# Loading six chunk numbers early and moving two small writes to ScalarE's queue at a loop's entry

## The chip, the cores and the metric

The kernel runs on one core of a Trainium2 chip. The metric is the device time of one execution in microseconds. Before the change three runs took 746.41, 743.29 and 744.07 us, median 744.07.

The core's engines each run their own list of instructions: TensorE (PE in the profile, with PEld for its weight loads), VectorE (DVE), ScalarE (ACT), GpSimd (POOL) and SyncE (SP). [...] An engine that issues a DMA spends about 0.3 us on it in its own list, and the list behind it waits as long. An engine meets another's results through semaphores, and so does the completion of a DMA reach the engines.

## The reference

Four graph layers work on one graph of N = 2708 nodes with 128 features each. Each layer normalises the rows (`h = max(layernorm(x), 0)`) and adds the layer's result to x. The adjacency matrix `adj` holds zeros and ones.

- Layer 0 is an attention layer with weights `adj.T * exp(max(0.2 C, C))`, divided by their sum in each row.
- Layer 1 is a graph convolution with symmetric degree scaling.
- Layer 2 is a mean over neighbours with a second linear map and a batch norm.
- Layer 3 decides here. With `XW = h @ W` and scores `s_col`, `s_row` of its rows:

```
den = exp(leaky_relu(s_row[:, None] + s_col[None, :], 0.01))
num = adj @ den
att = where(num != 0, den / num, 0)
out = x + adj @ (att @ XW)
```

`adj @ den` is a product of two matrices of 2708 x 2708. Since `den` depends on a sum of two scores through a function of two slopes, sorting the nodes by score turns most of each row of `num` into two prefix sums.

## The kernel before

The kernel first reads the adjacency matrix and its transpose as float32, packs them to 8 bits (`adj8_d`, `adjt8_d` in DRAM) and computes layers 0 to 2 with TensorE. Columns are worked on in six blocks of 512 (`E0`, the last has 148).

**Ranking and the sums' stage.** For layer 3 the nodes are ranked by score and split into NC = 22 chunks of CH = 124. The stage around lines 1246 to 1630 sums the adjacency rows of each chunk with weights (`sums`, `last_sums`), turns these sums into prefix sums over the chunks (`prefixes`, `flatten`) and stores them in two parts (`pre_hi`, `pre_lo`). The columns are done in three pairs of blocks, (0, 3), (1, 4) and (2, 5). `store_pre(i)` handles pair i: four writes into the small tensor `early_d[i]` (line 1524), four into the full tensor `pre_d` (line 1530), and then four reads from `early_d[i]` (line 1535) that put the prefix rows straight into the first two row tiles of the loop. Of the four early writes, h = 0 go to SP's queue and h = 1 to ScalarE's.

**Row tiles.** A row tile `r` of the loop (44 in all, number q) has 128 partitions. 124 hold adjacency rows, fetched by an indirect DMA on POOL's queue (`fetch_into`, line 1445) as 8 bits and widened by VectorE (`widen`, line 1479). The last four hold prefix rows from the chunk before it. Which chunk that is is known only on the device: `chunk_of(q)` (line 1459) loads the number from the tile `pre_i` into a register of SP, computes with it and asserts its bounds, and the DMA that follows takes its address from the register. For q = 0 and 1 this is done in the sums' stage (`first_chunks`). For q from 2 on `fetch_pre(q)` (line 1682) does it, each time right ahead of the read of `pre_d`.

**The loop.** Its 22 steps s use row tiles 2s and 2s + 1. In each, TensorE multiplies densities (`d_hi`, `d_lo`) by the two row tiles, one block of columns after the other (line 1737), ScalarE takes the logarithm (`ln`, line 1738) and inverts it (line 1705), VectorE forms `e` (line 1711), and two steps later TensorE multiplies `e` by the fetched `xw` (line 1693). Step 0 takes its blocks in the order 0, 3, 1, 4, 2, 5, as the pairs come. At the end of step s the row tiles 2s + 6 and 2s + 7 are fetched. Row tiles 2 to 5 have their prefix rows fetched ahead of the loop. Their gathers differ: 2 and 3 are fetched in the sums' stage, 4 and 5 inside step 0 after its third block, since VectorE first copies their indices (line 1748).

**The proof tiles.** The kernel also verifies that the adjacency matrix holds only zeros and ones. For that it reads it tile by tile into `chk` (line 699) and compares on VectorE (line 695). In the loop one such tile is read in each odd step, by ScalarE's queue after the third block, and compared in the next even step, ahead of later work of VectorE.

**Order.** The instructions of the sums' stage run on each engine in the order written (`in_order`), and in the loop the marked ones (`pin`) do. The order between the engines' DMAs, and which of a small set of completion semaphores each one gets, is fixed when the program is built.

Of the kernel before, what the change touches and what calls it, by code (L numbers as in the profile page):

```python
# [20 lines left out]
def binary(  # L21
# [21 lines left out]
    nc = tc.nc  # L43
# [1412 lines left out]
    def chunk_of(q):  # L1456
        traced = nc.cur_bb.bb.instructions
        n = len(traced)
        chunk_before = nc.sync.value_load(pre_i[0:1, q : q + 1], min_val=0, max_val=NC - 1)
        load = traced[n]  # L1460
        issued = next(i for i in reversed(traced[:n]) if i.engine == load.engine and "DMA" in type(i).__name__)
        tc.add_manual_dep(
            load,
            issued.name,
            mybir.DependencyInfo(mybir.DependencyClass.NoSync, mybir.DependencyReason.DATA),
            reason="chunk_of",
        )
        return chunk_before
# [3 lines left out]
    def fetch_into(q, pool):  # L1472
        g = pool.tile([P, N], U8, tag="g8", name="g8", bufs=4 if pool is rows8_pool else 2)
        pin(gather(g[:CH], adjt8_d[:, :], row_i2[:CH, q - 4 : q - 3] if q in (4, 5) else row_i[:CH, q : q + 1]))
        rows8[q] = g
# [4 lines left out]

    for q in range(4):
        fetch_into(q, rows8_pool)
    first_chunks = [chunk_of(q) for q in range(2)]
    for q in range(2):
        rows_r[q] = plan.tile([P, N], F32R, tag="wide3", name="r", bufs=3)

# [28 lines left out]
    def store_pre(i):  # L1515
        pair = (i, i + 3)
        pre_hi = merge.tile([P, 512], F32, tag="pre_hi", name="pre_hi", bufs=2)
        pre_lo = merge.tile([P, 512], F32, tag="pre_lo", name="pre_lo", bufs=2)
        ts_(pre_hi[:W108].bitcast(I32), flat[:W108].bitcast(I32), -4096, None, ALU.bitwise_and)
        nc.vector.tensor_sub(pre_lo[:W108], flat[:W108], pre_hi[:W108])  # L1520
        parts = [(o, h, part_sb) for o, part_sb in ((0, pre_hi), (2 * NC, pre_lo)) for h in range(2)]
        wide = [E0[b][1] - E0[b][0] for b in pair]
        for o, h, part_sb in parts:
            (nc.scalar if h else nc.sync).dma_start(
                early_d[i][o : o + 2 * NC, h * 512 : h * 512 + wide[h]].bitcast(F32),
                part_sb[64 * h : 64 * h + 2 * NC, : wide[h]],
            )
        for o, h, part_sb in parts:
            lo, hi = E0[pair[h]]
            nc.sync.dma_start(pre_d[o : o + 2 * NC, lo:hi].bitcast(F32), part_sb[64 * h : 64 * h + 2 * NC, : wide[h]])  # L1530
        early_rows = early_d[i].rearrange("(f c) n -> f (c n)", c=NC).bitcast(F32)
        for q in range(2):
            for h, b in enumerate(pair):
                lo, hi = E0[b]
                nc.sync.dma_start(
                    rows_r[q][CH:, lo:hi].bitcast(F32),
                    early_rows[:, bass.ds(first_chunks[q] * 1024 + h * 512, hi - lo)],
                )
# [40 lines left out]
    with in_order():  # L1579
# [20 lines left out]
        diagonal(0)  # L1600
        flatten(0, p0)
        store_pre(0)
        last_sums(1)
        p = bank()
# [14 lines left out]
        flatten(1, p1)  # L1619
        last_sums(2)  # L1620
        store_pre(1)
        evacuate(2)
        cp4 = spread_c(4)
# [4 lines left out]
        nc.scalar.activation(sig, c_tab, AF.Exp, scale=0.99)  # L1628
        flatten(2, p2)
        store_pre(2)  # L1630

    prep.close()
# [42 lines left out]
    def fetch_pre(q):  # L1675
        if q % 6 < 2:
            r = plan.tile([P, N], F32R, tag="wide3", name="r", bufs=3)
        else:
            r = steps.tile([P, N], F32R, tag="r", name="r", bufs=4)
        rows_r[q] = r  # L1680
        chunk_before = chunk_of(q)
        pin(nc.sync.dma_start(r[CH:, :].bitcast(F32), pre_rows[:, bass.ds(chunk_before * N, N)]))

    def fetch_xw(s):
# [13 lines left out]
    for q in range(2, 6):  # L1698
        fetch_pre(q)
# [16 lines left out]
    for s in range(NE):  # L1716
# [45 lines left out]
        for q in (2 * s + 6, 2 * s + 7):  # L1762
            if q < NS:
                fetch_pre(q)
# [460 lines left out]
def kernel(tc, *args):  # L2225
    nc = tc.nc
    with tc.tile_pool(name="verdict", bufs=1) as verdict:
        flag = verdict.tile([1, 1], I32, name="flag")
        binary(tc, flag, *args)
        other = nc.values_load(flag[0:1, 0:1], min_val=0, max_val=1, skip_runtime_bounds_check_because="0 or 1")  # L2230
        with tc.If(other > 0, preferred_fallthrough_block=False):
            general(tc, *args)
# [32 lines left out]
```

## Time and profile before

| What | Value |
|---|---|
| Median of three runs | 744.07 us |
| Profiled execution, its own time | 746.78 us |
| Profiled execution, span of its instructions | 744.9 us |
| TensorE busy | 654.9 us (88%) |
| VectorE busy | 584.5 us (78%) |
| ScalarE busy | 467.6 us (63%) |
| Mean granted TensorE clock | 0.962 |
| DMA traffic | 146.99 MB, 197 GB/s in the mean |

The page divides the span into 40 slices. The loop's entry lies in slices 23 to 26 (from about 428 us). The chain of waits goes back from the last instruction to what released it, at each step. A line of a timeline gives the start, the duration, the engine with a q where its queue only issues, the line of the kernel, the operation, what it writes and reads, and how many were merged. A waits line gives who waited for what: microseconds in total, how many times, and the longest. A windows line gives a stretch, its length, each engine's busy time, the granted clock, the share of the 16 DMA engines in use and the rate.

### The profile page before, as it was taken

The page shows a single profiled execution, that of the slowest core. Times are in us where ns is not written, and L with a number is a line of the kernel's source. Part 1 is how long each engine was busy: PE and PEld are TensorE (multiplying, and loading weights), DVE is VectorE, ACT ScalarE, POOL GpSimd, SP SyncE. Part 2 cuts the span into 40 slices and gives each one's busy share as a digit, 9 for nine tenths or more (in the row PEclk, how much of TensorE's full clock was granted, in tenths as well). Part 3 has the DMA queues.
Part 4 walks back from the last instruction along what each step waited for, and adds up shares of the span by engine and source line. Part 5 has one row for each costly group of instructions (what it writes and reads, how often), then busy time and mean ns, then how long its engine had stood idle before and what let it go on. Part 6 is the DMA issues. An engine that isn't in the chain of part 4 may idle for free.

```text
span 744.9 us, 8701 instructions
## 1 busy us (share of the span) xinstructions
PE 654.9 (88%) x2777; PEld 418.3 (56%) x2777; DVE 584.5 (78%) x1021; ACT 467.6 (63%) x694; POOL 218.0 (29%) x198
## 2 busy tenths in 40 slices
PE   6889888868899988866898976899999999999994
PEld 4433333415678766644455634556666666657784
DVE  5999968967876896654799974499789989858972
ACT  5765667648775653426575455668888888765442
POOL 3320000131110210004570427156666766000000
PEclk9999998999999999997999997989999999999998
DMA  9699999766731699600100248857887777568702
GB/s 336 253 384 416 424 428 399 265 242 220 292 119 71 204 305 349 208 0 14 44 22 2 65 128 134 174 153 153 180 176 170 174 173 169 151 220 330 260 30 57
DMA packets 49131, 146.99 MB, mean 197 GB/s; under 512 B 12686, under 2 KB 26930, under 8 KB 40658
## 3 DMA queue, kind: packets, MB, share of 16 engines
q1 hardware_dynamic: 29740, 87.76, 34.5%
q10 hardware_dynamic: 4714, 34.68, 14.0%
q0 software_dynamic: 14624, 23.92, 13.1%
q8 instruction: 24, 0.39, 0.2%
q14 instruction: 29, 0.24, 0.1%
HBM read 126.55 MB, written 19.73 MB: 196 GB/s over the span
## 4 chain that ended last, share of the span: by engine, by line
PE 48%; issue 15%; DVE 13%; DMA 9%; ACT 6%; POOL 2%; SPq 0%; ACTq 0%; POOLq 0%; DVEq 0%
PE bank L1737 13%; PE acc L1693 12%; PE acc L614 7%; PE acc L1860 5%; DMA chk<-in_adj_t_dram 4%; PE acc L1252 3%; DVE chk L695 2%; DMA adj_d<-a 2%; DVE m L483 2%; ACT adjt L216 2%; PE acc L1117 1%; ACT y L474 1%; POOL adj_d L372 1%; DVE r L1479 1%; POOL rstd L157 1%
## 5 line engine op out<-in xcount | busy, mean ns | idle before, releaser
L1737 PE MATMUL bank<-r,d_hi 128*128 128x512 f32 (+1 forms) x264 | 143.1, 546 | 14.7 <-DMA r<-pre_d 6.5
L1693 PE MATMUL acc<-e,xw 128*128 128x512 f32 (+1 forms) x264 | 121.8, 549 | 0.0
L1738 ACT ACTIVATE ln<-bank,tiny 128x512 f32<-128x512 f32 x132 | 83.9, 636 | 57.6 <-PE bank L1737 47.1
L340 PE MATMUL acc<-tau,hw 128*128 128x512 f32 (+1 forms) x240 | 99.7, 562 | 13.2 <-DVE tau L348 13.2
L1445 POOL DMA_INDIRECT g<-adjt_d,row_i x44 | 93.2, 2117 | 30.9 <-DVE r_hi L1439 10.7
L1737 PE MATMUL bank<-r,d_lo 128*128 128x512 f32 (+1 forms) x264 | 100.3, 385 | 0.0
L481 ACT CAST m<-a 128x660 fp32r<-128x660 fp8e4 (+1 forms) x45 | 55.2, 1234 | 51.7 <-PE acc L1860 30.7
L340 PEld LDWEIGHTS acc<-tau,hw 128*128 128x128 f32 x240 | 43.5, 193 | 71.2 <-issue 43.9
L695 DVE SCALAR_TENSOR_TENSOR chk<-chk 128x2708 f32<-128x2708 f32 (+1 forms) x22 | 65.5, 2978 | 21.4 <-DMA chk<-in_adj_t_dram 21.4
L348 DVE SCALAR_TENSOR_TENSOR tau<-row_b,sg,a 128x1536 f32<-128x1536 f32 (+1 forms) x44 | 70.8, 1623 | 13.3 <-DMA a<-in_adj_dram 13.2
L1711 DVE SCALAR_TENSOR_TENSOR e<-row_b,sig,ln 128x1536 f32<-128x1536 f32 (+3 forms) x46 | 71.4, 1558 | 11.2 <-PE bank L1737 8.3
L1737 PEld LDWEIGHTS bank<-r,d_hi 128*128 128x128 f32 x264 | 51.5, 195 | 51.1 <-issue 27.0
L1479 DVE CAST r<-g 124x2708 fp32r<-124x2708 fp8e4 x44 | 70.9, 1651 | 7.5 <-DMA r<-pre_d 7.5
L371 ACT ACTIVATE a<-a 128x2708 fp8e4<-128x2708 f32 x22 | 54.1, 2458 | 25.5 <-issue 13.3
L1737 PEld LDWEIGHTS bank<-r,d_lo 128*128 128x128 f32 x264 | 51.6, 196 | 29.2 <-issue 24.0
L1705 ACT ACTIVATE ln<-ln 128x512 f32<-128x512 f32 (+2 forms) x68 | 62.9, 927 | 0.7 <-ACT ln L1738 0.7
L157 POOL TENSOR_TENSOR rstd<-isq,neg_half 128x4 f32<-128x4 f32 (+1 forms) x24 | 28.8, 1200 | 117.4 <-DVE isq L156 73.3
L1445 POOL DMA_INDIRECT xw<-xw_d,xw_i x22 | 35.9, 1631 | 70.4 <-PE acc L1693 57.4
L483 DVE CAST m<-a 128x2048 fp32r<-128x2048 fp8e4 (+1 forms) x43 | 39.5, 920 | 21.3 <-PE acc L614 11.7
L1693 PEld LDWEIGHTS acc<-e,xw 128*128 128x128 f32 x264 | 48.4, 191 | 12.8 <-issue 3.8
L614 PE MATMUL acc<-m,y_hi 128*128 128x512 f32 (+1 forms) x132 | 50.8, 391 | 4.8 <-ACT m L481 1.9
L614 PE MATMUL acc<-m,h_hi 128*128 128x512 f32 (+1 forms) x132 | 53.8, 415 | 0.1
(449 smaller groups left out, 1237.0 us busy)
## 6 DMA issues: line engine op xcount, KB each, us to landing
a<-in_adj_dram SPq DMA_DIRECT2D x21, 1354.0 KB
adjt<-in_adj_t_dram ACTq DMA_DIRECT2D x12, 1354.0 KB
chk<-in_adj_t_dram ACTq DMA_DIRECT2D x11, 1354.0 KB
chk<-in_adj_t_dram SPq DMA_DIRECT2D x10, 1354.0 KB
a<-in_adj_t_dram SPq DMA_DIRECT2D x9, 1354.0 KB
adj_d<-a POOLq DMA_DIRECT2D x22, 338.5 KB, 8.3
adjt_d<-adjt SPq DMA_DIRECT2D x5, 1354.0 KB
a<-adj_d SPq DMA_DIRECT2D x5, 1024.0 KB
```

Source lines behind the costliest of these rows:

```text
L340: nc.tensor.matmul(accs[b][:, : hi - lo], stationary, tau[b // 3][:, o : o + hi - lo], start=first, stop=last)
L348: nc.vector.scalar_tensor_tensor(tau, row_b[:, h0:h1], sg[:, t : t + 1], tiles_a[t][:, h0:h1], ALU.max, ALU.mult)
L481: nc.scalar.copy(m[:, : hi - lo], src[:, lo:hi])
L614: nc.tensor.matmul(sums_of[phase, b][:, : hi - lo], part[:, t, :], tiles_m[k][:, lo - base : hi - base], start=t == 0 and i == 0, stop=t = ...
L695: lambda: nc.vector.scalar_tensor_tensor(a[:r], a[:r], 1.0, a[:r], ALU.is_equal, ALU.not_equal, accum_out=odd[:r, t : t + 1])
L1445: return nc.gpsimd.indirect_dma_start(out=out, out_offset=None, in_=src, in_offset=bass.IndirectOffsetOnAxis(ap=idx, axis=0),)
L1479: pin(nc.vector.tensor_copy(rows_r[q][:CH], g[:CH]))
L1693: m = nc.tensor.matmul(ys_acc[b][:, : hi - lo], xws[s], waiting[s][:, lo:hi], start=(s == 0), stop=(s == NE - 1))
L1705: pin(nc.scalar.activation(lns[s][:, lo:hi], lns[s][:, lo:hi], AF.Exp, scale=-1.0))
L1711: nc.vector.scalar_tensor_tensor(waiting[s][:, lo:hi], row_b[:, lo:hi], sig[:, s : s + 1], lns[s][:, lo:hi], ALU.max, ALU.mult)
L1737: pin(nc.tensor.matmul(num[:, : hi - lo], d, a[:, lo:hi], start=(j == 0), stop=(j == 3)))
L1738: pin(nc.scalar.activation(lns[s][:, lo:hi], num[:, : hi - lo], AF.Ln, bias=tiny))
```

## The change

Six chunk numbers, not two, are loaded into SP's registers in the sums' stage, behind the last DMA that SP issued before and after `pre_i` is ready. `fetch_pre` for row tiles 2 to 5 uses these registers and loads nothing. All four early writes of the third column pair are issued by ScalarE; those of the first two pairs stay as they were.

```
@@ -1480,7 +1480,7 @@
     for q in range(4):
         fetch_into(q, rows8_pool)
-    first_chunks = [chunk_of(q) for q in range(2)]
+    first_chunks = [chunk_of(q) for q in range(6)]
     for q in range(2):
         rows_r[q] = plan.tile([P, N], F32R, tag="wide3", name="r", bufs=3)
@@ -1521,7 +1521,7 @@
         for o, h, part_sb in parts:
-            (nc.scalar if h else nc.sync).dma_start(
+            (nc.scalar if h or i == 2 else nc.sync).dma_start(
                 early_d[i][o : o + 2 * NC, h * 512 : h * 512 + wide[h]].bitcast(F32),
                 part_sb[64 * h : 64 * h + 2 * NC, : wide[h]],
             )
@@ -1678,7 +1678,7 @@
         rows_r[q] = r
-        chunk_before = chunk_of(q)
+        chunk_before = first_chunks[q] if q < 6 else chunk_of(q)
         pin(nc.sync.dma_start(r[CH:, :].bitcast(F32), pre_rows[:, bass.ds(chunk_before * N, N)]))
```

More of the change, by code (lines that the diff above doesn't have):

```diff
@@ L1482, in binary @@
         fetch_into(q, rows8_pool)
-    first_chunks = [chunk_of(q) for q in range(2)]
+    first_chunks = [chunk_of(q) for q in range(6)]
     for q in range(2):
@@ L1523, in store_pre @@
         for o, h, part_sb in parts:
-            (nc.scalar if h else nc.sync).dma_start(
+            (nc.scalar if h or i == 2 else nc.sync).dma_start(
                 early_d[i][o : o + 2 * NC, h * 512 : h * 512 + wide[h]].bitcast(F32),
@@ L1680, in fetch_pre @@
         rows_r[q] = r
-        chunk_before = chunk_of(q)
+        chunk_before = first_chunks[q] if q < 6 else chunk_of(q)
         pin(nc.sync.dma_start(r[CH:, :].bitcast(F32), pre_rows[:, bass.ds(chunk_before * N, N)]))
```

## The prediction

> **What bounds the kernel now.** I read the page's slices first, then the chain of waits where the loop starts, the windows of the loop's steps, and the waits of SP's queue.
>
> From 500 us on, the loop of 22 steps is TensorE's own: a step takes 9.64 us without idle time. The change touches nothing there, so what counts is when step 5 starts (499.63). The chain of waits just before (start, length, what):
>
> ```profile
> 445.00 1.59 DMA r<-early_d
> ...
> 446.64 0.76 PE bank L1737 x2
> ...
> 447.55 0.49 SPq L1459
> ...
> 448.52 6.82 DMA r<-pre_d
> 455.48 1.21 PE bank L1737 x2
> ...
> 459.77 20.54 DMA chk<-in_adj_t_dram
> ...
> 485.05 2.97 DVE r L1479 x2
> 488.06 1.22 PE bank L1737 x2
> ```
>
> The reader is to see three links. A chunk load (L1459) stands ahead of row tile 3's read of `pre_d`; that read, issued at 448.52, takes 6.8 us, and step 1 waits for it until 455.48. ScalarE issues the transfer of the proof tile `chk` in the middle of step 1, at 459.77. It lands at 480.3, and VectorE then needs 7.7 us (L695, `e`, two widenings) until step 4 runs in full at 488.06.
>
> The windows of steps 1 to 5, matmuls of L1737 alone:
>
> ```profile
> core 0: us, PE busy (x) PEld busy (x), PEclk, DMA share, GB/s
> ...
> 450.30:462.40 12.10, 8.02 (x24) 5.44 (x24) 0.64 0.90 152
> 463.20:472.85 9.65, 8.12 (x24) 4.29 (x25) 1.00 1.07 192
> 472.85:485.20 12.35, 7.82 (x24) 4.22 (x24) 1.00 0.80 157
> 486.60:499.63 13.03, 10.55 (x24) 5.21 (x25) 0.75 0.60 172
> 499.63:509.27 9.64, 8.13 (x24) 4.32 (x25) 1.00 0.49 123
> ```
>
> Step 2 is a clean 9.65; steps 3 and 4 lose 7.5 us together, against 2 x 9.63 from 472.85 to a possible 492.1. Step 4 also runs at clock 0.75. The DMA engines are full meanwhile (0.90, 1.07).
>
> SP's queue, around the change (start, length, what):
>
> ```profile
> 438.08 3.33 SPq L1535 DMA_DIRECT2D r<-early_d  x4
> 441.51 0.31 SPq L1524 DMA_DIRECT2D early_d<-pre_hi  x1
> 441.91 0.31 SPq L1524 DMA_DIRECT2D early_d<-pre_lo  x1
> 442.27 0.73 SPq L1530 DMA_DIRECT2D pre_d<-pre_hi  x2
> 443.05 0.75 SPq L1530 DMA_DIRECT2D pre_d<-pre_lo  x2
> 444.06 1.99 SPq L1535 DMA_DIRECT2D r<-early_d  x4
> 447.22 4.23 SPq L1682 DMA_DIRECT2D r<-pre_d  x4
> ```
>
> The four last reads take 4.23 us because each has a chunk load in front of it. What SP waits for, in total, how often, the longest:
>
> ```profile
> SPq L1682 <- DMA chk<-in_adj_t_dram: 15.2, 1, 15.2
> ...
> SPq L1535 <- DMA early_d<-pre_hi: 1.7, 1, 1.7
> ```
>
> Neither reader needs that data: the trace shows SP's and ScalarE's DMAs taking turns on eight completion semaphores, and a DMA that gets one in use waits. Moving two writes to ScalarE can therefore move a wait on SP.
>
> **The change, part by part.**
>
> *Four chunk loads earlier.* The loads for q = 0 and 1 stand at 415.37 and 416.18 and are over at 416.78: 0.81 and 0.60 us each, made of the load itself (0.28 to 0.46), its address (0.15) and an assertion (0.02). Four more take 2.4 to 3.2 us, to 420 at the latest. SP's next work is at 429.03, after a wait of 12.2 us for `pre_hi`: cover enough, cost nothing. If that cover were gone they would cost these 3.2 us. The change issues no more DMAs in all.
>
> *The same four loads gone from the entry.* The spacing of the four reads is 1.30 us (448.52 to 449.81); without load, address and assertion (0.81 us) it is 0.47. So row tile 2 is read 0.9 us sooner and row tile 3 1.7 us sooner, apart from the next edit.
>
> *Two early writes of the third pair off SP.* They took 441.51 to 442.27, so what follows moves 0.76 us forward. They go out on ScalarE at 438.70 and 439.4 rather than 441.5 and 441.9, so their data is there before SP reads it. ScalarE pays two issues of 0.30 us: the first in the stretch where it waits for `pre_lo` (438.70 to 439.06), the second ahead of step 0's first logarithm, 439.43 to 439.77. Behind that stands TensorE's third block, 440.17 to 440.5, which stops until 442.25 anyway for a read of the second pair. Cost nothing; without that stop, 0.34 us. VectorE has no new wait; POOL's queue is passed by nothing.
>
> *The semaphore turns.* One of the second pair's reads waits 1.7 us, to 440.7, for a third-pair write on ScalarE. With four such writes the first read may wait too. Bounds: no wait at all (1.7 us gained) and all four reads behind 440.7 (438.08 becomes 440.7, and the last ends 0.9 us later). I take 0.5 us of loss, nearer the second, since the one wait that shows is of that sort. So the gathers of row tiles 4 and 5, released by step 0's third block at 446.5, go at 447.0. They have slack: both are widened by 461.2, and step 2 started at 463.24.
>
> *Step 1.* Row tile 3's read goes at 448.52 - 1.7 - 0.76 + 0.5 = 446.6. It needs the writes of `pre_d`, whose last is issued at 443.2 and takes the 2.3 us that an early write takes in the chain (435.55 to 437.88): 445.5, no stop. How long does it take? Row tile 2's read took 3.1 us (447.22 to TensorE's 450.32), before gather packets filled the engines; row tile 3's took 6.8, among them. Ends: 449.7 and 453.4. At 446.6 it is ahead of the gathers, so I take 449.7 to 450. Step 1 is then 5.5 us sooner (2.1 at the other end).
>
> *The transfer of `chk`.* Its issue follows step 1: 459.77 - 5.5 = 454.3. The landing moves by 0 to 5.5 us: nothing if the engines, at a share of 0.85 or more from 452 us on, have no room; 5.5 if it lands as long after its issue. I take 3.5, since the packets of its queue took 65% of the engines between 464 and 472 us and the gathers' 29%: where it competes, it wins. It lands at 476.8. [...]
>
> *Step 4.* VectorE's 7.7 us after the landing gives 484.5 in place of 488.06: 3.5 us. Without a late transfer, step 4 can start when step 3 ends, at 482.5: 5.5 us.
>
> *The clock.* From 488.06 to 499.63 step 4 needed 11.57 us, 1.9 more than a warm step: half clock after TensorE's idling between 482 and 488. With some 2 us idle instead of 5 I take 1.4 of it back (ends 0 and 1.9). [...] The window after 452 us, at 0.50, agrees that idling costs clock.
>
> **Sum.** 0 (early loads) + 0 (ScalarE) + 3.5 + 1.4 = 4.9 us, all of it at step 5's start; from there the loop and the last product run as before. The profiled execution took 746.78 us by its own time (span 744.9 and 1.9 around it), 2.7 above the median of the three runs, 744.07. So 741.9 for that execution, and 744.07 - 4.9 = 739.2 as the forecast. About 0.5% (3.7 us) is what a measurement tells from no change.
>
> **Rivals.**
>
> *The gain stays in the entry.* Step 1 starts early, but `chk` lands 0 to 2 us sooner, because the DMA engines are full from 452 to 480 us. For it: shares 0.85 to 1.15 in those windows. [...] Also here: row tile 3's read is slow wherever it goes (6.8 us), which moves step 1 by 2.1 only. Time 744.07 - 0 to 2.5, say 742.5.
>
> *Slower: the early `chk` starves the gathers of row tiles 4 and 5.* They land 11.1 to 11.5 us after issue now; the slowest of the eight, issued among the transfer's packets, needed 23.8. Today the transfer's packets come after 462 us, when these two have landed (458.0 and 459.3). From 456 us they would run into them. With 23.8 us, tile 5 lands at 471.5 or later, is widened by 474.6, and step 2 starts 11.4 us late. Step 5 then starts at 474.6 + 3 x 9.64 = 503.5, 3.9 later than now: 748.0. It decides from 469 us on for tile 5's landing; sooner than that the step-4 stall that goes pays for it. Against it: they are nearly done by 457.
>
> *The change does not do what it says.* The waits list also holds one of TensorE (0.2 us) for row tile 2's read at 447.4; were it real, that read stays at 447.2 and tile 3's comes at 447.7. It would still be 0.8 us sooner, 743 or a little less.
>
> **How the numbers follow.** Forecast (3.7 us or more gained): 0.55, own range 735.5 to 740.3, the low end being 5.5 + 1.9 and another 1.2 from steps 2 and 3 moving forward. Gain stays in the entry: 0.22; the change does not do what it says: 0.05. Slower by starved gathers: 0.18. These give the chances of faster, same (0.22 + 0.05) and slower. The range, 735.5 to 746.0, leaves out some 0.05 below and about 0.13 of the slow case above.
>
> **What would show it.** Right: the four reads of L1682 within 2 us from about 446; step 1's full start near 450; the `chk` issue near 454; step 3 without a stop, step 4 at clock 0.9 or more, step 5's start near 494.7. Wrong: `chk` landing at 479 or later; a long stop at step 2 behind widening (starved gathers); SP stopped before the second pair's reads beyond 441.5.

## The result and the profile after

The changed kernel takes 755.76 us (median of four runs, 750.76 to 758.33) where the kernel before takes 744.21 in the same comparison: a ratio of 1.0128, 95% interval 1.0087 to 1.017. It is slower by about 1.3%; the forecast was 739.2 and its range ended at 746.0. A ratio leaves out executions that took over 1.5% more than the fastest of the same kernel; this concerns kernel 11 below alone, where it leaves out three of ten.

The profiled execution took 753.69 us by its own time (span 751.8), 6.9 more than the one before. The loop begins 1.8 us earlier in this trace, and the loop's entry loses 8.5 us: counted from the first matmul of L1737, step 5 starts at 71.8 us in place of 63.3, and from there to the end it is 245.4 us in one trace and 245.3 in the other. Below, "at t = ..." means microseconds after that first matmul (434.52 in this trace, 436.33 before).

The windows of step 0 to step 5, matmuls of L1737 alone, in the changed kernel (columns as before):

```profile
core 0: us, PE busy (x) PEld busy (x), PEclk, DMA share, GB/s
434.52:448.83 14.31, 8.73 (x24) 5.63 (x25) 0.76 0.35 98
448.83:457.29 8.46, 7.53 (x24) 5.21 (x24) 0.80 0.89 130
457.29:466.37 9.08, 0.00 (x0) 0.03 (x1) 0.68 1.04 217
466.37:487.11 20.74, 10.88 (x24) 5.34 (x25) 0.65 0.47 83
487.11:496.73 9.62, 8.12 (x24) 4.31 (x25) 1.00 0.50 115
496.73:506.36 9.63, 8.13 (x24) 4.31 (x25) 1.00 0.90 171
```

Step 1 is what the change promised: 8.46 us instead of 12.10. Steps 3 and 4 are clean at 9.62 and 9.63, without the stop that the proof tile caused before. Everything is lost between them: 9.08 us in which TensorE multiplies nothing, and a step 2 of 20.74 us. Step 2 pays for the stop twice: between 461 and 481 us the granted clock is 0.50.

What step 2 waits for stands in the chain of waits of the changed kernel:

```profile
446.08 1.30 POOL g L1445
...
447.69 25.68 DMA g<-adjt_d,row_i
473.44 1.58 DVE r L1479
475.06 1.22 PE bank L1737 x2
```

It is the gather of row tile 5, which takes 25.7 us after its issue. In the kernel before, the gathers of row tiles 4 and 5 stand so among the DMA issues (the last number is the microseconds from issue to landing):

```profile
g<-adjt_d,row_i POOLq DMA_INDIRECT x1, 11.5
```

```profile
g<-adjt_d,row_i POOLq DMA_INDIRECT x1, 11.1
```

VectorE's widenings in the changed kernel show that row tile 4 is late too (in brackets the idle time ahead of each, and what ended it):

```profile
464.70 1.57 DVE L1479 CAST r<-g 124x2708 fp32r<-124x2708 fp8e4 x1 [14.64 <-DMA g<-adjt_d,row_i]
473.44 1.57 DVE L1479 CAST r<-g 124x2708 fp32r<-124x2708 fp8e4 x1 [7.17 <-DMA g<-adjt_d,row_i]
```

Row tile 4 was issued at 446.08 and landed at 464.6, which is 18.5 us against 11.5 before. These are two delays, the second landing 8.7 us behind the first, and the experiments are about what makes each. SP's queue and POOL's around them in the changed kernel, then POOL's in the kernel before:

```profile
439.30 1.62 SPq L1535 DMA_DIRECT2D r<-early_d  x4
441.02 0.70 SPq L1530 DMA_DIRECT2D pre_d<-pre_hi  x2
441.85 0.69 SPq L1530 DMA_DIRECT2D pre_d<-pre_lo  x2
443.06 1.65 SPq L1535 DMA_DIRECT2D r<-early_d  x4
445.04 1.65 SPq L1682 DMA_DIRECT2D r<-pre_d  x4
446.74 0.37 SPq L1668 DMA_DIRECT2D c_row<-ctwo_d  x1
448.13 1.75 SPq L1682 DMA_DIRECT2D r<-pre_d  x2
```

```profile
446.08 1.30 POOL L1445 DMA_INDIRECT g<-adjt_d,row_i  x1 [8.96 <-DVE row_i L1748]
447.69 1.30 POOL L1445 DMA_INDIRECT g<-adjt_d,row_i  x1 [0.30 <-issue]
```

```profile
446.51 1.30 POOL L1445 DMA_INDIRECT g<-adjt_d,row_i  x1 [7.37 <-DVE row_i L1748]
448.12 1.29 POOL L1445 DMA_INDIRECT g<-adjt_d,row_i  x1 [0.30 <-issue]
```

The issue of each of these gathers keeps POOL for 1.29 or 1.30 us; SP's reads of `pre_d` and ScalarE's early writes took 0.28 to 0.34 us each in the kernel before.

The four reads of row tiles 2 to 5 now go out in 1.65 us (4.23 before), and the transfer into `c_row`, 128 KB, follows right behind. All five are issued before POOL has finished issuing the gather of row tile 4, at 447.38. What the DMA engines then did between 448 and 452 us, before any packet of the proof tile, first in the kernel before, then in the changed one (packets, MB, share of the 16 engines):

```profile
q0 software_dynamic: 399, 0.32, 33.1%
q1 hardware_dynamic: 8, 0.04, 4.4%
```

```profile
q1 hardware_dynamic: 171, 0.20, 45.9%
q0 software_dynamic: 350, 0.06, 20.8%
```

q0 is POOL's queue (the gathers), q1 is SP's. In these four microseconds the gathers moved 0.32 MB before and 0.06 MB now; SP's transfers moved 0.04 MB before and 0.20 MB now, with 45.9% of the engines' time in place of 4.4%.

### The profile page after: what moved, and what is told of

Read it like the earlier page. It is cut to its first block, busy times and chain, and to the rows that moved or that the text cites. A ratio compares the mean times of both kernels' runs of the same rounds, so it can differ in the third digit from the quotient of the medians.

```text
span 751.8 us, 8698 instructions
## 1 busy us (share of the span) xinstructions
PE 656.2 (87%) x2777; PEld 419.1 (56%) x2777; DVE 583.6 (78%) x1021; ACT 467.8 (62%) x694; POOL 221.0 (29%) x198
## 4 chain that ended last, share of the span: by engine, by line
PE 49%; issue 14%; DVE 12%; DMA 9%; ACT 6%; POOL 3%; SPq 0%; ACTq 0%; POOLq 0%; DVEq 0%
PE bank L1737 14%; PE acc L1693 14%; PE acc L614 6%; PE acc L1860 5%; DMA g<-adjt_d,row_i 3%; PE acc L1252 3%; DVE chk L695 3%; DMA chk<-in_adj_t_dram 2%; DMA adj_d<-a 2%; ACT adjt L216 2%; DVE m L483 2%; PE acc L1117 1%; ACT y L474 1%; POOL rstd L157 1%; POOL adj_d L372 1%
## 5 line engine op out<-in xcount | busy, mean ns | idle before, releaser
L1737 PE MATMUL bank<-r,d_hi 128*128 128x512 f32 (+1 forms) x264 | 144.0, 550 | 23.1 <-issue 9.1
L340 PE MATMUL acc<-tau,hw 128*128 128x512 f32 (+1 forms) x240 | 101.6, 572 | 12.2 <-DVE tau L348 12.1
L1445 POOL DMA_INDIRECT g<-adjt_d,row_i x44 | 91.8, 2086 | 47.4 <-DVE r L1479 15.5
L1737 PE MATMUL bank<-r,d_lo 128*128 128x512 f32 (+1 forms) x264 | 100.9, 387 | 0.0
L1479 DVE CAST r<-g 124x2708 fp32r<-124x2708 fp8e4 x44 | 70.4, 1639 | 21.8 <-DMA g<-adjt_d,row_i 21.8
L1737 PEld LDWEIGHTS bank<-r,d_hi 128*128 128x128 f32 x264 | 52.0, 197 | 58.2 <-issue 29.9
L340 PEld LDWEIGHTS acc<-tau,hw 128*128 128x128 f32 x240 | 44.5, 197 | 71.2 <-issue 45.9
L371 ACT ACTIVATE a<-a 128x2708 fp8e4<-128x2708 f32 x22 | 54.1, 2458 | 24.6 <-issue 11.8
L1737 PEld LDWEIGHTS bank<-r,d_lo 128*128 128x128 f32 x264 | 52.0, 197 | 29.6 <-issue 24.5
L1445 POOL DMA_INDIRECT xw<-xw_d,xw_i x22 | 40.3, 1831 | 59.5 <-PE acc L1693 49.1
L1693 PEld LDWEIGHTS acc<-e,xw 128*128 128x128 f32 x264 | 48.4, 191 | 12.8 <-issue 3.8
L483 DVE CAST m<-a 128x2048 fp32r<-128x2048 fp8e4 (+1 forms) x43 | 39.5, 919 | 19.7 <-PE acc L614 10.1
```

Source lines behind the costliest of these rows:

```text
L340: nc.tensor.matmul(accs[b][:, : hi - lo], stationary, tau[b // 3][:, o : o + hi - lo], start=first, stop=last)
L1445: return nc.gpsimd.indirect_dma_start(out=out, out_offset=None, in_=src, in_offset=bass.IndirectOffsetOnAxis(ap=idx, axis=0),)
L1479: pin(nc.vector.tensor_copy(rows_r[q][:CH], g[:CH]))
L1693: m = nc.tensor.matmul(ys_acc[b][:, : hi - lo], xws[s], waiting[s][:, lo:hi], start=(s == 0), stop=(s == NE - 1))
L1737: pin(nc.tensor.matmul(num[:, : hi - lo], d, a[:, lo:hi], start=(j == 0), stop=(j == 3)))
```

## The experiments

Two theories were on record when the first kernels ran. **P**, the slow rival of the prediction: the proof tile's transfer, now 3 to 5 us earlier, starves the gathers. **R**: SP's reads crowd them, either the four of row tiles 2 to 5 (R1) or those of row tiles 6 and 7, which now follow 2 us behind (R2).

**1 and 2. Each half of the change alone.** The chunk loads alone:

```
-            (nc.scalar if h or i == 2 else nc.sync).dma_start(
+            (nc.scalar if h else nc.sync).dma_start(
```

> The chunk part of the change alone: six chunk numbers loaded early, the third pair's writes divided between SP and ScalarE as before. Two theories of the loss. P (proof transfer): the transfer of chk, now issued 5 us sooner, takes the DMA engines from the gathers of row tiles 4 and 5. R (reads): without the chunk loads between them, SP's reads of pre_d for row tiles 2 to 7 stand in a row ahead of the gathers of tiles 4 and 5 and already hold them up before chk comes. Both expect this kernel slow, 750 to 757 us, with the gather of row tile 5 landing 20 us or more after its issue, since the 0.8 us per read is the larger part of what SP gains. If instead the moved writes carry the loss, it is 743 to 745 us.

Measured: 751.78 us, ratio 1.0085 (1.0063 to 1.0108). The writes alone:

```
-    first_chunks = [chunk_of(q) for q in range(6)]
+    first_chunks = [chunk_of(q) for q in range(2)]
...
-        chunk_before = first_chunks[q] if q < 6 else chunk_of(q)
+        chunk_before = chunk_of(q)
```

> The writes' part alone: the third pair's four early writes on ScalarE, the chunk loads of row tiles 2 to 5 where they were. SP gains 0.76 us there, and the second pair's first read may wait for the third pair's writes as in the changed kernel. P and R both expect 743 to 745.5 us, no change that can be told, with the gathers of row tiles 4 and 5 landing 11 to 13 us after issue. If the writes carry the loss: 752 or more.

Measured: 740.33 us, ratio 0.9925 (0.9893 to 0.9957), below what both theories expected. The loss belongs to the chunk loads, and the writes' half is a gain that the change buried: a kernel faster than both. Windows of its steps 0 to 4:

```profile
437.27:451.83 14.56, 8.63 (x25) 5.74 (x25) 0.77 0.30 89
451.83:462.68 10.85, 8.18 (x25) 6.00 (x25) 0.69 0.89 156
462.68:473.20 10.52, 8.38 (x25) 4.25 (x25) 1.00 1.06 211
473.20:484.82 11.62, 7.83 (x25) 4.24 (x25) 1.00 0.97 164
484.82:497.05 12.23, 9.58 (x25) 4.79 (x25) 0.86 0.80 189
```

Step 5 starts at t = 59.8 (63.3 before). Step 1 is 2.1 us shorter than before (10.85 against 12.92, from first matmul to first matmul), although its reads go out 0.6 us later: the gather of row tile 4 is issued 1.5 us later (t = 11.7, 10.2 before), and row tile 3's read, now issued 0.1 us ahead of the end of POOL's issue, takes 4.1 us instead of 6.8. The proof tile is issued at t = 21.7 (23.4) and lands at 41.2 (44.0).

**3. The proof tile later.** The whole change, with the first proof tile of the loop read in step 2 and compared in step 3:

```
-                if s and s % 2 == 0:
+                if s > 2 and s % 2 == 0 or s == 3:
                     pin(check())
-                if s % 2:
+                if s % 2 and s > 1 or s == 2:
```

> The changed kernel with the loop's first proof transfer issued in step 2 and compared in step 3, in place of steps 1 and 2; all later ones as before. P: with chk out of the way the gather of row tile 4 lands 11 to 13 us after issue and that of tile 5 before 462 us; step 2 runs from 461 on, and the time is 744 us or less. R: the gather of tile 4 still lands 17 to 19 us after its issue (464), since that was so before a packet of chk moved; tile 5 lands near 467 rather than 473; time 745 to 750 us.

Measured: 753.25 us, ratio 1.0102 (1.0059 to 1.0145). VectorE's widenings of row tiles 4 and 5:

```profile
467.66 3.05 DVE L1479 CAST r<-g 124x2708 fp32r<-124x2708 fp8e4 x2 [14.04 <-DMA c_row<-ctwo_d]
```

It starts at t = 29.8 and both row tiles are widened back to back. (The releaser named is a transfer that ended at about the same time; the gather itself lands at t = 29.7.) So the gather of row tile 5 lands 0.6 us after that of row tile 4 (t = 30.3 and 29.7), where the changed kernel has 38.8 and 30.1. P is right for the second delay, the 8.7 us of row tile 5, and wrong for the first: row tile 4 is as late (17.9 us) with no proof tile in flight. The time hardly improves, because the proof tile now disturbs later steps:

```profile
481.52:494.62 13.10, 7.82 (x25) 4.21 (x25) 1.00 0.53 122
494.62:505.85 11.23, 9.31 (x25) 4.96 (x25) 0.85 0.66 190
```

Steps 3 and 4 cost 5.1 us more than two of 9.62.

**4 and 5. The reads of row tiles 6 and 7 later.** The first try moved their code into step 1's fourth block:

```
+                if s == 1:
+                    for q in (6, 7):
+                        fetch_pre(q)
```

> The changed kernel with the reads of pre_d for row tiles 6 and 7 issued after step 1's fourth block in place of the end of step 0; they are needed in step 3 only. P: nothing changes for the gathers of tiles 4 and 5, the latter lands past 470 us; 753 to 757 us. R: two of the reads that compete with the gather of tile 4 are gone, it lands 12 to 15 us after issue (458 to 461), tile 5 sooner as well; time 744 to 750 us.

Measured: 754.9 us, 1.0132 (1.0095 to 1.017), but SP runs ahead of TensorE and issued the reads only 0.8 us later, at t = 14.4 and 15.9 (13.6 and 15.1): no test of R2. It also moved the second transfer into `c_row` forward, to t = 12.9 from 15.4, and the gather of row tile 4 took 22.8 us. The second try makes SP spend time on six chunk loads that nobody uses:

```
+        if q == 6:
+            for _ in range(6):
+                chunk_of(q)
```

> The changed kernel with six extra chunk loads on SP, whose numbers nothing uses, between the c_row fetch after row tile 5's read and the read for row tile 6: a pause of 5 us. (The earlier attempt to issue the reads of tiles 6 and 7 later did not delay them, as SP runs ahead.) Theory R in two forms. R1: the four reads for tiles 2 to 5, bunched within 1.4 us ahead of the gather of tile 4, hold it up; that is unchanged here, it still lands 16 us or more after issue; 750 us or more. R2: it is the reads for tiles 6 and 7, which the change brings ahead of that gather's data; here they go at 452 or later and it lands 11 to 14 us after issue; 746 us or less.

Measured: 755.2 us, 1.012 (1.0078 to 1.0162). The reads go out 3.4 us later (t = 17.0 and 18.5), and the gather of row tile 4 is not faster; its line among the DMA issues:

```profile
g<-adjt_d,row_i POOLq DMA_INDIRECT x1, 19.6
```

R2 falls.

**6. The same pause ahead of row tile 4's read.** The reads of row tiles 2 and 3 stay early.

```
+        if q == 4:
+            for _ in range(6):
+                chunk_of(q)
```

> The changed kernel with the same pause between the reads for row tiles 3 and 4. Tiles 2 and 3, which step 1 needs, are read as early as in the changed kernel, the others at 450 us or later, after the gather of tile 4 has begun. R1 and R2 both: that gather lands 11 to 14 us after issue, step 1 runs from 450 on, time 736 to 743 us. If it stays over 750, the bunching of SP's reads is not the cause, and the early start of step 1 itself is.

Measured: 742.45 us, 0.9934 (0.9908 to 0.996). Adding 4 us of useless work to SP gives back more than the whole loss. The gather of row tile 4 there:

```profile
g<-adjt_d,row_i POOLq DMA_INDIRECT x1, 7.8
```

It takes 7.8 us, against 18.5. The proof tile is as early as in the changed kernel (issued at t = 19.6) and does these gathers no harm: both have landed by t = 25.7, and the first packet of its queue comes at 25.8. The gather came in even sooner than the 11 to 14 us expected.

**7. Only the chunk numbers of row tiles 2 and 3 early.**

```
-    first_chunks = [chunk_of(q) for q in range(6)]
+    first_chunks = [chunk_of(q) for q in range(4)]
...
-        chunk_before = first_chunks[q] if q < 6 else chunk_of(q)
+        chunk_before = first_chunks[q] if q < 4 else chunk_of(q)
```

> The change with four chunk numbers loaded early instead of six: row tiles 2 and 3 are read without loads between them, tiles 4 and 5 with their loads, 1.3 us apart. R1: the gather of tile 4 meets two reads in a row and two spaced ones; it lands 12 to 15 us after issue, time 738 to 746 us. R2: the reads for tiles 6 and 7 go some 2 us later than in the changed kernel, not enough; 746 to 752 us.

Measured: 743.55 us, 0.9959 (0.9927 to 0.9991). Gather of row tile 4 in 10.7 us, sooner than the 12 to 15 expected of R1; step 5 at t = 58.9.

**8. Pause and late proof tile together.** The edits of 6 and 3.

> The pause between tiles 3 and 4 together with the first proof transfer one step later. P says that the transfer of chk costs the gathers of tiles 4 and 5 time whenever it is issued near 454: this one is then 2 us or more faster than with the pause alone. If P plays no part once the gathers come in time, the two agree within 2 us, or this one is slower, since its transfer now ends in step 3.

Measured: 750.36 us, 1.0043 (1.0015 to 1.0072). The gather takes 7.3 us, but the proof tile read in step 2 lands in step 3's way (14.7 us): step 5 starts at t = 65.0 instead of 59.5. With the gathers on time, the early proof tile is the better place.

**9 and 10. Closeness or order?** A pause ahead of row tile 2's read keeps the four reads as close together as in the change, but puts them behind the gather's issue. Loading the numbers of row tiles 4 and 5 alone early keeps three of them close, most of them behind it.

```
+        if q == 2:
+            for _ in range(6):
+                chunk_of(q)
```

> The changed kernel with the same pause of SP (six unused chunk loads, 4.2 us in the kernel that pauses ahead of row tile 4's read) ahead of row tile 2's read, so that all four reads still go out within 1.5 us of each other, but 3 us behind the gather of row tile 4 in place of 1 us ahead of it. It asks what makes the four reads harmful. Bunching: four reads so close together hold up the gathers wherever they stand; the gather of row tile 4 again takes 16 to 19 us (18.5 in the changed kernel), step 5 starts 71 us or more after step 0's first matmul, and the time is 753 or more. Order: only reads issued before the gather's packets are on their way hold it up; the gather then takes 7 to 12 us (7.9 with the pause ahead of row tile 4's read). Step 1 now has to wait up to 4.1 us longer for row tile 2's read, so the time lies between 742.5 (the kernel with the pause ahead of row tile 4) and 746.6 on that account.

> The changed kernel with the chunk numbers of row tiles 4 and 5 alone loaded early (those of 2 and 3 have their loads at the reads, as before). The four reads then stand at about 11.3, 12.6, 13.05 and 13.5 us after step 0's first matmul, the gather of row tile 4 is issued at 11.5. The reads of row tiles 3 to 5 are as close together as in the changed kernel, but behind the gather's issue. Bunching: the gather of row tile 4 takes 14 us or more, step 5 starts at 65 or later, time 747 to 751. Order: the gather takes 10 to 12 us, as in the kernel before (11.5) and in the one with the chunk numbers of row tiles 2 and 3 alone early (10.7), step 5 starts at 58 to 61, and the time is 740 to 744.5.

The second kernel's edit:

```
-    first_chunks = [chunk_of(q) for q in range(6)]
+    first_chunks = {q: chunk_of(q) for q in (0, 1, 4, 5)}
...
-        chunk_before = first_chunks[q] if q < 6 else chunk_of(q)
+        chunk_before = first_chunks[q] if q in first_chunks else chunk_of(q)
```

Measured: 747.27 us, 1.0017 (0.999 to 1.0045), and 743.11 us, 0.9958 (0.9927 to 0.9989). The gather of row tile 4, in the first and then in the second kernel:

```profile
g<-adjt_d,row_i POOLq DMA_INDIRECT x1, 12.7
```

```profile
g<-adjt_d,row_i POOLq DMA_INDIRECT x1, 11.9
```

So it is order and not closeness alone, although 12.7 is a little above the 12 that was written down (in that kernel POOL spent 2.3 us on the gather's issue, not 1.3). Four reads ahead of the gather but spaced out were not tried. The first kernel pays for its late reads in step 1 (step 2 starts at t = 32.2), as expected of it: its median is 0.7 above the upper bound.

**11. Three reads early.** The fourth, row tile 5's, has its load at the read.

```
-    first_chunks = [chunk_of(q) for q in range(6)]
+    first_chunks = [chunk_of(q) for q in range(5)]
...
-        chunk_before = first_chunks[q] if q < 6 else chunk_of(q)
+        chunk_before = first_chunks[q] if q < 5 else chunk_of(q)
```

> The changed kernel with the chunk numbers of row tiles 2, 3 and 4 early and that of row tile 5 loaded at its read, so that three reads stand ahead of the gather of row tile 4 (at about 10.5, 10.9 and 11.3 us; gather at 11.5) and the fourth comes at 12.6. With two reads ahead that gather took 10.7 us, with four ahead 18.5. In the four-read kernels the reads finish 1.6 us after one another. If each read ahead costs the gather its own time and some crowding behind it, three ahead give 12 to 16 us, step 5 starts between 60 and 68 us after step 0's first matmul and the time lies between 744 and 752. If it is a matter of the fourth read alone (its row tile 5's, next to the second gather), the gather takes 11 us or less and the time is 742 to 745. If three ahead are as bad as four, the gather takes 18 us and the time is 752 or more.

Measured: 749.84 us median of ten, but from 741.71 to 757.76; the ratio is 1.0002 (0.9967 to 1.0036), but the spread says more here. In the traced execution (753.03 us, the third longest of the ten) the gather took 19.0 us, as with four reads ahead. SP's four reads and the gather's issue there:

```profile
446.23 2.53 SPq L1682 DMA_DIRECT2D r<-pre_d  x4
```

```profile
447.27 1.30 POOL L1445 DMA_INDIRECT g<-adjt_d,row_i  x1 [8.34 <-DVE row_i L1748]
```

The fourth read was issued at 448.46, and POOL's instruction ended at 448.57, 0.1 us later. That no expectation fits all ten executions agrees with a race, but only one of them was traced. Nor is it shown that the fourth read decided: the transfer into `c_row` goes out right behind it, at t = 12.7, where kernel 7 has it at 13.9.

**12. The transfer into `c_row` later.** In all kernels so far it came right behind row tile 5's read and moved with it.

```
+        if s0 == 8:
+            for _ in range(6):
+                chunk_of(0)
         nc.sync.dma_start(p, ctwo_d[s0 * P : (s0 + 2) * P].partition_broadcast(P))
```

> The changed kernel with the pause of SP (six unused chunk loads, 4.2 us) between the read of row tile 5 and the transfer of 128 KB into c_row that stands behind it in the queue. In every kernel so far that transfer came right behind the read of row tile 5, so it moved together with the reads and could be the cause in their place. Reads: the four reads alone, still at 10.5 to 11.9 us after step 0's first matmul, hold up the gather of row tile 4; it takes 17 us or more (18.5 in the changed kernel), and the time is 751 or more. c_row and the reads of row tiles 6 and 7: all three now go out 4 us later, behind the gather; it takes 8 to 12 us, step 5 starts at 58 to 62, and the time is 740 to 745. Row tile 5 is not known to go the same way: with the proof tile's transfer still early it may be late by itself, so the gather of row tile 4 decides.

Measured: 749.24 us, 1.0037 (1.001 to 1.0063). The gathers of row tiles 4 and 5 among the DMA issues:

```profile
g<-adjt_d,row_i POOLq DMA_INDIRECT x1, 14.2
```

```profile
g<-adjt_d,row_i POOLq DMA_INDIRECT x1, 22.3
```

14.2 us lies between the two expectations; read so, both have a part. With `c_row` (and the reads of row tiles 6 and 7) behind the gather, 4.3 us of the 18.5 go. With the reads of row tiles 4 and 5 behind it as well (kernel 6) another 6.4 go. The reads of row tiles 6 and 7 alone (kernel 5) are worth nothing. These are single traces, and the traced execution of kernel 12 is the slowest of its ten (757.19 us, the others 747.62 to 753.47), so how the delay divides is an estimate.

**All kernels side by side.** POOL's issue of row tile 4's gather ends 1.3 us after it starts (2.3 in kernel 9), and the first packet of POOL's queue comes 0.6 to 0.9 us after that end. The table counts how many of the four reads were issued by that end; in kernels 1, 2 and 11 one read is counted that went out 0.1 us ahead of it. Times are t in us; "`c_row`" is the issue of the first transfer into it, "5 lands" is row tile 5's gather.

| Kernel | reads issued | `c_row` | gather's issue ends | reads ahead | gather 4 takes | 5 lands | step 5 | ratio |
|---|---|---|---|---|---|---|---|---|
| before | 10.9, 12.2, 13.5, 14.8 | 15.2 | 11.5 | 1 | 11.5 | 22.9 | 63.3 | 1 |
| after | 10.5, 11.0, 11.4, 11.9 | 12.2 | 12.9 | 4 | 18.5 | 38.8 | 71.8 | 1.0128 |
| 1 loads alone | 10.1, 10.6, 11.0, 11.5 | 11.8 | 11.6 | 4 | 17.8 | 37.9 | 69.6 | 1.0085 |
| 2 writes alone | 11.5, 12.9, 14.2, 15.5 | 15.9 | 13.0 | 2 | 11.8 | 24.7 | 59.8 | 0.9925 |
| 3 late proof | 10.7, 11.2, 11.6, 12.1 | 12.4 | 13.1 | 4 | 17.9 | 30.3 | 68.0 | 1.0102 |
| 4 reads 6, 7 moved | 10.8, 11.3, 11.7, 12.2 | 12.5 | 13.2 | 4 | 22.8 | 40.6 | 72.7 | 1.0132 |
| 5 pause at 6 | 10.5, 10.9, 11.4, 11.9 | 12.2 | 12.8 | 4 | 19.6 | 39.5 | 72.1 | 1.012 |
| 6 pause at 4 | 10.6, 11.0, 15.2, 15.7 | 16.0 | 13.0 | 2 | 7.8 | 25.7 | 59.5 | 0.9934 |
| 7 two early | 10.5, 10.9, 12.2, 13.5 | 13.9 | 12.8 | 3 | 10.7 | 26.6 | 58.9 | 0.9959 |
| 8 pause at 4, late proof | 10.5, 11.0, 15.1, 15.7 | 16.0 | 12.9 | 2 | 7.3 | 26.7 | 65.0 | 1.0043 |
| 9 pause at 2 | 13.9, 14.4, 14.8, 15.3 | 15.6 | 13.5 | 0 | 12.7 | 30.6 | 65.0 | 1.0017 |
| 10 last two | 11.4, 12.7, 13.2, 13.7 | 14.0 | 12.9 | 2 | 11.9 | 27.7 | 59.4 | 0.9958 |
| 11 three early | 10.1, 10.6, 11.0, 12.3 | 12.7 | 12.5 | 4 | 19.0 | 37.9 | 69.7 | 1.0002 |
| 12 `c_row` later | 10.4, 10.8, 11.3, 11.8 | 15.8 | 12.8 | 4 | 14.2 | 35.4 | 68.4 | 1.0037 |

With all four reads ahead the gather takes 14 to 23 us; with three or fewer, 7 to 13, and within those the count doesn't order them (7.8 with two ahead, 12.7 with none). One rival stays inside the rule: in every kernel with four reads ahead but one, the transfer into `c_row` goes out by t = 12.7, at most 0.3 us behind the end of the gather's issue, and in all others at 13.9 or later. Kernel 12 alone separates the two. That SP's transfers, when they go first, hold up the gather is shown; how much of it is the reads' and how much `c_row`'s rests on that one trace.

The early proof tile was taken away twice. With the reads ahead (kernel 3 against the changed one) row tile 5's gather lands 8.5 us sooner by it; with the gathers on time (kernel 8 against 6) it lands 1.0 us later.

## Why the prediction was wrong

**Right: the entry.** The early loads cost nothing. The four reads stand 0.44 to 0.52 us apart (0.47 predicted). Row tile 3's read landed at 450.2 (449.7 to 450 predicted). The proof tile was issued at 454.54 (454.3) and landed at 472.0, even sooner than the 476.8 predicted, and steps 3 and 4 ran without a stop, at clock 1.00. That last point tests nothing here, since step 3 began 15 us after the landing. Some of the early times lie in the profiled execution, whose loop began 1.8 us earlier: measured from the first matmul, the issue came 3.4 us sooner, not 5.5. Kernel 7 comes near a test of the rest of the sum: the proof tile is as early there, the gather of row tile 4 is on time, steps 3 and 4 take 9.62 and 9.63 us, and step 5 starts 4.4 us sooner than before, where the sum gave 4.9.

**Mis-sized: the semaphore turns.** I took 0.5 us of loss. SP's reads of the second pair wait 2.3 us for a write's semaphore (1.7 before):

```profile
SPq L1535 <- DMA early_d<-pre_hi: 2.6, 2, 2.3
```

They all stand behind it. Step 0's third block is done 1.4 us later (its logarithm starts at t = 8.6 instead of 7.2), and the gather that it releases goes out at t = 11.6 instead of 10.2. That is beyond the bound of 0.9 that I gave, and it put the gather still further behind the reads. The loss does not need it: in kernel 1 the gather goes at 10.3 and takes 17.8 us.

**The step that failed: "They have slack: both are widened by 461.2".** I moved the gathers by 0.5 us and kept their durations, 11.1 to 11.5 us; they took 18.5 and 25.7. In the next paragraph I used that the read of row tile 3 "is ahead of the gathers" to make the read shorter, which came true, and never asked what the reads then do to the gathers. The trace of before had the pair of prices to ask it with: 3.1 us for a read ahead of the gathers, 6.8 among them. A read that is slow among the gathers may slow them when it goes first. The sum had no term for it, and that term is the result: row tile 4's gather takes 7.0 us longer and row tile 5's, which the early proof tile then meets, 14.6. It is no fixed exchange: in kernel 7 row tile 3's read takes 4.8 us and the gather only 10.7.

**The slow rival was half right.** It named the gathers and the stall at step 2 and gave 748.0; tile 5 landed at 473.4, past the 469 from which it was to decide. But its mechanism, the proof tile, makes only the second half. Its own counterargument, "they are nearly done by 457", comes near the truth when the reads do not all go first: in kernels 6, 7 and 10 the proof tile is just as early or nearly so (issued at t = 19.6 to 21.3; 20.0 in the change), and row tile 5's gather lands at 25.7 to 27.7 rather than 38.8. Its sum also took step 2 at full clock: from row tile 5's widening on, step 2 needed 12.05 us (475.06 to 487.11), not 9.64. Taken alone, with the reads ahead and no early proof tile, the reads' part is kernel 3: 17.9 us for row tile 4's gather, step 5 at t = 68.0.

**The proof tile's landing.** I took 476.8, since between 464 and 472 us the packets of its queue had taken 65% of the engines and the gathers' 29%, and 479 or later as a sign against me. It came at 472.0, 17.4 us after its issue (20.5 before), while the gathers were held up. From its issue to its landing its queue had 29.7% of the engines and the gathers' 59.8% (36.5% and 54.0% in the kernel before), so the two shares that I went by do not account for the sooner landing. How the engines divide their time among the queues no run shows.

**Time.** The trace accounts for 8.5 us at step 5's start (6.9 by the executions' own times). The medians differ by 11.5 us. The other three executions of the changed kernel (750.76, 757.83 and 758.33, at mean granted clocks of 0.960, 0.947 and 0.949; the traced one had 0.952) were not traced, so their share in this is open.

## What to carry to other kernels

A gap in a queue can be what lets another queue's transfer in: here some 4 us of it ahead of row tile 4's read brought that row tile's gather from 18.5 to 7.8 us. Before removing useless-looking work ahead of DMAs, list who else issues in the same few microseconds, who leaves first then, and which of them is the critical one. When a price in a trace depends on who came first (3.1 us ahead, 6.8 among), swapping the order can charge the other side (here the gather, 18.5 us in place of 11.5), so give that side its own term.

## What the runs showed of the hardware

In both traces VectorE starts to widen row tile 4 right after the last of its gather's 16 completion events. In the changed kernel 12 of them come by t = 19.3 and the last four at 29.4 to 30.1; the widening starts at 30.2. In the kernel before, the twelve come by t = 13.8 and the last four at 18.7 to 21.7; the widening starts at 21.8. With the transfer into `c_row` issued later (kernel 12) it starts at t = 25.8. Each of the changed kernel's reads of `pre_d` for row tiles 2 to 5, which have four rows, shows one event 0.4 us after its issue and four later, and the four reads finish one behind the other, at t = 14.2, 15.7, 17.7 and 18.7, 1.0 to 2.0 us apart for 42.3 KB each.

Why the last four events of the gather come another 11 us after the fourth read has finished (t = 18.7 and 29.4 to 30.1 in the changed kernel) stays open. By kernel 12 `c_row` has some 4 us of the delay (14.2 us against 18.5). By what way the reads hold up the gather is not shown: the traces do not name the DMA engine of a packet.
